# A planned graph and LSTM kernel: weights folded behind the first batches, LSTM states carried through DRAM, buffers freed at a store's landing

## The chip, the cores and the metric

The kernel runs on one core of a Trainium2 chip. The metric is device time in microseconds. The core's engines are TensorE (PE), VectorE (DVE), ScalarE (ACT), GpSimd (POOL), and SyncE (SP), which here only issues DMAs, in order.

## The reference

Inputs are `x` (32 batches of 512 nodes with 128 features, f32), a symmetric 0/1 adjacency `adj` (32 x 512 x 512, ones on the diagonal), and weights. Each of four layers normalises its input over the features (`LN`), takes the relu, and its result is added to its input. Cut to what matters:

```
x1 = x  + softmax over neighbours of relu(q) . relu(k), times relu(v)      # attention
h  = relu(LN(x1));  dyn = conv(h[last 128 nodes]);  lw = LSTM(dyn)          # 128 steps, all batches
x2 = x1 + sigmoid( (D^-1/2 (A + I) D^-1/2 h) @ lw )
n  = relu(LN(x2));  four times: n_i = tanh( A_norm(n W_s..) , n W_n.. , A_norm(n W_d..) ; W_u )
x3 = x2 + n_4
out = x3 + prelu( A_norm (relu(LN(x3)) W^T) + bias )
```

The LSTM runs over 128 steps for all 32 batches at once, each step waiting for the one before. It needs the attention's result for the last 128 nodes of every batch, and the second layer of every batch needs its states `lw`. Since the adjacency is symmetric, the kernel multiplies `W_s`, `W_d`, `W_n` with the blocks of `W_u` beforehand; this product of weights is the *folding*.

## The kernel before

`symmetric` first describes the work as operations and then has a planner order them. There are three stages.

- **First pass** (`pass_1(b)`, ranks 10000 and up): per batch, `LN`, the projections to keys and values, the attention of the last 128 nodes and the convolution. Keys, values and the updated nodes are stored to DRAM (`f_dkq`, `f_dv`, `f_dl`). The convolution's result is written into `f_seq` (128 x 128 x 32).
- **LSTM stage**: `lstm()` has a chain per step: PE products into `f_z` (`L1252`, four quarter matmuls at a time, the "tiled" mode), tanh on ACT (`L1278`, `L1290`), the cell on DVE (`L1284`, `L1285`), tanh of the cell (`L1292`), then the state: `f_h` (`L1296`), transposed in 32 x 32 blocks into `f_seq` (`L1297`). Between the steps `pass_2(b)` does the attention of the other 384 nodes for batches 0 to 27 (`f_pq`, `f_s`, `f_po`). For batches in `EARLY` it loads the whole adjacency, squares it on ACT (`L1389`), forms the second layer's neighbour sums (`f_pg`, in `aggregate`, `L1451`) and stores them (`f_dgT`). Behind batches 4, 7, 10 and 13 of this pass `fold(i)` makes the folded weights of layer `i`.
- **Rest** (`rest(b, turn)`): per batch, the adjacency again, the second layer's gates (`f_pl`), the four message layers (`f_py` `L1548`, `f_pa` `L1451` and `L1559`), the last layer (`f_pg`, `f_p`), the output. The order of turns is `FIRST` (batches 26, 27, begun in the LSTM stage), `NEXT`, then the others by number. The last four batches' `pass_2` lies in this stage.

Before a batch's gates the state is turned: PE transposes `f_seq[:, :, b]` into a PSUM bank `f_plw` (`L1506`), and ACT or DVE copies it to `f_lw` with a factor of 0.5.

The planner (`Plan.run`) gives each operation an engine, a start and an end from costs written into the description, takes at each point the operation that can start first (lowest rank among equals), and emits the instructions in that order; each engine then runs its own in order. Buffers are counted pools (`BUFS`); a new cell has to wait until a slot is free (`free_at`, plus `HOP`). DMAs take their issue time on SP, and `gap` is the extra time until the data can be used. Instruction supply of PE is modelled too: an operation may not start before `FETCH` us after the instruction `AHEAD` places earlier, less `KEEP` places for work that is not an LSTM step:

```
            n = taken[-1] + o.count + (self.KEEP if o.rank >= self.URGENT and self.left else 0) - self.AHEAD
            ...
            return at_time[k] + self.FETCH - o.engines["PE"][0]
```

DMAs issued in the LSTM stage for ranks of 20000 and up also wait for the LSTM step that the plan put before them (`hold_back`).

Of the kernel before, what the change touches and what calls it, by code (L numbers as in the profile page):

```python
# [8 lines left out]
FP = mybir.dt.float32  # L9
AF = mybir.ActivationFunctionType  # L10
OP = mybir.AluOpType
# [510 lines left out]
class Plan:  # L522
# [14 lines left out]
    SWITCH = (0.28, 0.1)  # L537
    AHEAD, FETCH, KEEP = 264, 5.0, 32

# [30 lines left out]
    def op(self, engines, rank, reads=(), writes=(), after=(), gap=0.0, tiled=False, count=8):  # L570

        o = Op()
        o.engines, o.rank, o.no, o.gap = engines, rank, len(self.ops), gap
        o.tiled = tiled
        o.patience = 0.15
        o.count = count
        deps = set(after)
        cells = []
        for acc, is_write in [(a, False) for a in reads] + [(a, True) for a in writes]:
            c, part = acc if isinstance(acc, tuple) else (acc, None)  # L580
            if c not in cells:
                cells.append(c)
            for key, (ws, rs) in c.parts.items():
                if part is None or key is None or key == part:
                    deps.update(ws)
                    if is_write:
                        deps.update(rs)
            mine = c.parts.setdefault(part, ([], []))
            if is_write:
                c.parts[part] = ([o], [])  # L590
            else:
                mine[1].append(o)
        deps.discard(o)
        o.deps = list(deps)
        o.cells = [c for c in cells if c.pool is not None]
        for c in o.cells:
            c.left += 1
        self.ops.append(o)
        return o
# [9 lines left out]
    def run(self, tc, queues):  # L609
# [101 lines left out]
        while done < len(ops):  # L711
# [43 lines left out]
            for c in o.cells:  # L755
                if c not in seen:
                    seen.add(c)
                    slots[c.tag].remove(place(c, s) if c.tag == self.banks else min(slots[c.tag]))
                    if c.tag in self.fifo:
                        turn[c.tag] += 1  # L760
                c.left -= 1
                c.free_at = max(c.free_at, o.end)
                if c.left == 0:
                    slots[c.tag].append(c.free_at)
                    if c.tag == self.banks:
                        unused.append((c.free_at, c.place))
# [22 lines left out]
def symmetric(ctx, tc, x, adj, weights, cols, rows, lstm_b, prelu_a, out, fail):  # L789
# [20 lines left out]
    FIRST = [B - LATE - 2 + k for k in range(2)]  # L810
    NEXT = [22, 23]
    EARLY = range(22)
    FOLDS = (4, 7, 10, 13)
    MOVED = range(2, B - 2)
# [3 lines left out]
    LANDED = 3.8  # L818
    STORED = 5.0
    PATIENCE = 1.3  # L820
    plan_rest = 30_000
    assert D == P and N == 512

    BUFS = {"a": 2, "ar": 6, "x": 7, "xn": 5, "y": 5, "gs": 5, "inv": 4, "n0": 4, "n1": 4, "n2": 4, "n3": 4, "low": 3, "hp": 2, "dt": 2, "mm": 8, "st": 4, "mv": 4, "rs": 4, "sh": 4, "dg": 8, "dv": 4,
            "ri": 3, "th": 3, "c": 3, "cu": 2, "cv": 2, "tcn": 2, "h": 2}
    const = ctx.enter_context(tc.tile_pool(name="f_const", bufs=1))
# [103 lines left out]
    minus_alpha = const.tile([P, 1], FP, name="f_minus_alpha")  # L930
    lb = const.tile([P, 8, TURN], FP, name="f_lb")
    lb_row = const.tile([P, 4, TURN], FP, name="f_lb_row")
# [19 lines left out]
    w_crow = load(HEAD + 12, 64, conv_row, rows[R_CONV].partition_broadcast(P))  # L952
    w_lb = plan.fixed(lb)
    for j in range(P // TURN):
        part = bass.ts(j, TURN)
        DMA(HEAD + 100, 4, lambda part=part: nc.sync.dma_start(
            lb[part], lstm_b.rearrange("s q f -> (s q) f")[:, part].partition_broadcast(TURN)), [], [(w_lb, j)])
    w_lstm = load(HEAD + 100, 512, w[:, W_IH : W_SD[0], :], weights[:, W_IH : W_SD[0], :])
    sd_col = const.tile([P, R_U3 + 1 - R_SD], FP, name="f_sd_col")
    sd_cols = load(HEAD + 100, 5, sd_col, rows[R_SD : R_U3 + 1].rearrange("r p -> p r"))  # L960
    w_last = load(LAST, 64, w_fc, weights[:, W_FC, :])
# [42 lines left out]
    def two_biases():  # L1004
        nc.gpsimd.tensor_add(lb_row, lb[:, :4, :], lb[:, 4:, :])
        for gates in (slice(0, 2), slice(3, 4)):
            nc.gpsimd.tensor_scalar_mul(lb_row[:, gates, :], lb_row[:, gates, :], 0.5)
# [62 lines left out]

    def ln_rstd(rank, mv, a, b, rs):

        def fn():
            nc.gpsimd.tensor_scalar_add(rs[0](), mv.t[:, a:b, 1], EPS_LN)
            nc.gpsimd.tensor_tensor(rs[0](), rs[0](), neg_half[:, 0, a:b], OP.pow)
        POOL(rank, 0.78 + 0.13 * (b - a), fn, [mv], [rs[1]])

# [17 lines left out]

    def ln_full(rank, xc, name, relu=False):
        mv = ln_stats(rank, xc, range(NT), name)
        rs = new("rs", (P, NT), f"f_rs_{name}")
        ln_rstd(rank, mv, 0, NT, (lambda: rs.t[:, :], rs))
        sh = new("sh", (P, NT), f"f_sh_{name}")  # L1100
        ln_shift(rank, lambda: mv.t[:, :, 0], rs, sh, [mv])
        return ln_apply(rank, xc, lambda t: mv.t[:, t, 0:1], lambda t: rs.t[:, t : t + 1], lambda t: sh.t[:, t : t + 1],
                        [mv, rs, sh], name, relu)
# [40 lines left out]
    def pass_1(b):  # L1144
        R = 10_000 + b * 10
        xc = new("x", (P, NT, P), f"f_x_{b}")
        DMA(R, 256, lambda: nc.sync.dma_start(xc.t, x[b].rearrange("(t p) d -> p t d", p=P)), [], [xc],
            gap=2.0 if b == 0 else 4.5 if b < 4 else 3.5)
        al = new("n1", (P, NT, P), f"f_al_{b}")
        DMA(R + 11, 256, lambda: nc.sync.dma_start(al.t, adj[b, :, NR:].rearrange("(t p) i -> p t i", p=P)), [], [al])  # L1150
        xn = ln_full(R, xc, f"a{b}")


# [82 lines left out]


    def lstm():
        last = list(conv_ops)
# [21 lines left out]
        for t in range(T):  # L1261
# [30 lines left out]
            ACT(R, 0.13, lambda tcn=tcn, cn=cn: nc.scalar.activation(tcn.t, cn.t[:, 3, :], AF.Tanh, scale=0.5), [(cn, 2)], [tcn])  # L1292
            h = new("h", (P, TURN), f"f_h_{t}")

            def out_of(th=th, tcn=tcn, h=h, t=t):
                nc.vector.scalar_tensor_tensor(h.t, th.t[:, 4, :], 1.0, tcn.t, OP.add, OP.mult)  # L1296
                return nc.vector.transpose(seq[:, t, :], h.t)  # L1297
            last = [DVE(R, 0.35, out_of, [(th, 1), tcn], [h])]
            steps += last
# [7 lines left out]
    def pass_2(b):  # L1307
# [58 lines left out]
        if early:  # L1366
# [9 lines left out]
            dg = plan.fixed(dram.tile([P, N], FP, tag=f"g{b}", name=f"f_dgT_{b}"))  # L1376
            DMA(R + 5, 256, lambda: nc.sync.dma_start(dg.t, flat(gT.t)), [gT], [dg])
            kept_sums[b] = dg
# [14 lines left out]
    def turned_back(rank, b, a, ar, pieces):  # L1393
# [6 lines left out]
        for k in range(pieces):  # L1400
# [3 lines left out]
            def differ(k=k, at=at):  # L1404
                nc.vector.scalar_tensor_tensor(junk[:, : n * N], flat(a.t[:, n * k : n * (k + 1), :]), 1.0, flat(aT.t[:, n * k : n * (k + 1), :]),  # L1405
                                               OP.mult, OP.not_equal, accum_out=viol[:, at : at + 1])
# [40 lines left out]
    def aggregate(rank, parts, ar, pg):  # L1447
# [15 lines left out]
        return last  # L1463

    def rest(b, turn, lw_after):
        R = 30_000 + turn * 10
# [18 lines left out]
        def norms():  # L1485
# [3 lines left out]
            nc.gpsimd.tensor_tensor(d[:, 0:2, :], d[:, 0:2, :], neg_half, OP.pow)  # L1489
            nc.gpsimd.tensor_scalar_mul(d[:, 2, :], d[:, 0, :], 0.5)  # L1490
            nc.gpsimd.memset(d[:, 3:, :], 0.0)
# [4 lines left out]


        if b in EARLY:
            gT, first = new("gs", (P, N), f"f_gT3_{b}"), None
            gT.ahead = 2  # L1500
            DMA(R, 256, lambda: nc.sync.dma_start(gT.t, kept_sums[b].t), [kept_sums[b]], [gT])
        else:
            gT, first = sums_of_1(R, b, xc, ar, rs)
            diagonal(R, ar, OP.subtract)
        plw = bank(f"f_plw_{b}", (P, P), whole=False)
        PE(R, T_TR, lambda: nc.tensor.transpose(plw.t, seq[:, :, b], ident), [gT], [plw], after=lw_after + ([first] if first else []))  # L1506
        lw = new("low", (P, P), f"f_lw_{b}")
        evict(R, P, lambda: lw.t, lambda: plw.t, [plw], [lw], scale=0.5)
        pl = bank(f"f_pl_{b}", (P, NT, P))
# [11 lines left out]
        moved = turn in MOVED  # L1521
        xn = ln_full(R, xc, f"c2{b}", moved)

# [51 lines left out]
        if turn == B - 1:  # L1575
# [3 lines left out]
            [p4], [xc])  # L1579
        xd = ln_full(R, xc, f"d{b}")  # L1580

# [59 lines left out]
    sum_ops, differ_ops, late, differs = [], [], [], [0]  # L1641
    junk = const.tile([P, 2 * N], BF, name="f_junk")
    for b in range(B):
        pass_1(b)
    end = lstm()
    for b in range(B):
        pass_2(b)
        if b in FOLDS:
            fold(FOLDS.index(b), 20_000 + b * 10)
    for k, b in enumerate(FIRST + NEXT + [b for b in range(B) if b not in FIRST + NEXT]):  # L1650
# [88 lines left out]
```

## Time and profile before

| | us |
|---|---|
| median of 3 runs (1287.78, 1291.28, 1291.68) | 1291.28 |
| profiled execution, its own time | 1290.13 |
| its span, first to last instruction | 1288.3 |
| PE busy | 1259.9 (98%) |
| DVE busy | 985.2 (76%) |
| ACT busy | 834.1 (65%) |
| POOL busy | 386.9 (30%) |
| DMA moved | 232.03 MB, mean 180 GB/s |
| LSTM: first and last transpose into `f_seq` | 181.5 and 497.6 |

The granted TensorE clock was 0.998 in the mean. A busy share is a mean over stages; PE's is besides made from modelled ends of matmuls, which overlap with what follows.

### The profile page before, as it was taken

Reading aid. Unit: us, or ns where it says so; the run is one execution under the profiler, and the core shown is the slowest. Engines: PE = TensorE matmul, PEld = TensorE weight load, DVE = VectorE, ACT = ScalarE, POOL = GpSimd, SP = SyncE. Lnnn points to the kernel's source line nnn. Section 1 sums busy time; section 2 is a strip of 40 time slices with the busy share of each in tenths; the row PEclk is TensorE's granted clock in tenths of the full one; section 3 lists DMA queues with packets and bytes.
Section 4 is the critical chain, followed back from the end, with each engine's and each line's share of the span. In section 5 each row is a group of like instructions: output and inputs, shape, how many; then the busy total and the mean of one; then the engine's idle time right before and its main releaser. Section 6 shows DMA issues by size and latency. Waiting matters only on the chain.

```text
span 1288.3 us, 33017 instructions
## 1 busy us (share of the span) xinstructions
PE 1259.9 (98%) x12085; PEld 971.5 (75%) x12085; DVE 985.2 (76%) x3279; ACT 834.1 (65%) x2092; POOL 386.9 (30%) x733
## 2 busy tenths in 40 slices
PE   8999999999999999999999999999999999999997
PEld 6888876666666667877778787787877877877774
DVE  7889878888878889876677676776776767887654
ACT  5666658777776757764576666666766765676433
POOL 4654523222213216421223232232232322332000
PEclk9999999999999999999999999999999999999999
DMA  8888888868748995877477777776766655673211
GB/s 263 272 273 285 263 263 285 263 208 285 228 138 288 243 272 151 191 165 163 85 164 159 152 164 161 164 150 152 163 162 149 170 116 110 128 173 70 54 25 36
DMA packets 300795, 232.03 MB, mean 180 GB/s; under 512 B 140752, under 2 KB 246224, under 8 KB 300624
## 3 DMA queue, kind: packets, MB, share of 16 engines
q1 hardware_dynamic: 283728, 213.06, 59.9%
q0 software_dynamic: 16896, 16.78, 8.5%
q8 instruction: 97, 1.59, 0.5%
q14 instruction: 74, 0.61, 0.1%
HBM read 136.19 MB, written 62.13 MB: 154 GB/s over the span
## 4 chain that ended last, share of the span: by engine, by line
PE 86%; DVE 7%; ACT 2%; DMA 2%; POOL 1%; issue 1%; DVEq 0%; ACTq 0%; SPq 0%; POOLq 0%
PE f_pa L1451 18%; PE f_py L1548 15%; PE f_pa L1559 15%; PE f_pg L1451 8%; PE f_s L1343 5%; PE f_z L1252 4%; PE f_po L1349 4%; PE f_p L1600 2%; PE f_pk L1159 2%; PE f_pv L1175 2%; PE f_pl L1513 2%; PE f_pol L1202 2%; PE f_sl L1192 2%; PE f_pd L1227 1%; PE f_pq L1334 1%
## 5 line engine op out<-in xcount | busy, mean ns | idle before, releaser
L1451 PE MATMUL f_pa<-f_ar,f_y 128*128 128x512 f32 x1024 | 299.3, 429 | 0.0
L1451 PEld LDWEIGHTS f_pa<-f_ar,f_y 128*128 128x128 f32 x1024 | 189.7, 188 | 73.9 <-issue 40.2
L1548 PE MATMUL f_py<-f_wf,f_n 128*128 128x128 f32 x1280 | 174.0, 275 | 0.0
L1548 PEld LDWEIGHTS f_py<-f_wf,f_n 128*128 128x128 f32 x1280 | 165.3, 191 | 9.4 <-issue 1.9
L1559 PE MATMUL f_pa<-f_n,f_wf 128*128 128x512 f32 x320 | 153.2, 593 | 0.1
L1563 ACT ACTIVATE f_n<-f_pa,f_bcol 128x512 f32<-128x512 f32 x128 | 88.3, 690 | 98.1 <-PE f_pa L1559 98.1
L1434 ACT CAST f_y<-f_py 128x512 fp32r<-128x512 f32 x128 | 74.9, 585 | 95.2 <-PE f_py L1548 90.4
L1389 ACT ACTIVATE f_ar<-f_a 128x512 fp32r<-128x512 f32 x216 | 133.7, 622 | 3.7 <-DMA f_a<-in_adj_dram 2.4
L1396 POOL DMA_DIRECT2D f_das<-f_ar x32 | 26.9, 842 | 350.1 <-ACT f_ar L1389 293.2
L1555 DVE TENSOR_TENSOR f_pa<-f_pa,f_inv 128x512 f32<-128x512 f32 x128 | 86.5, 692 | 28.5 <-PE f_pa L1451 28.3
L1349 PE MATMUL f_po<-f_v,f_e 128*32 128x129 f32 x3072 | 107.4, 273 | 0.4 <-DVE f_e L1347 0.2
L1349 PEld LDWEIGHTS f_po<-f_v,f_e 128*32 128x32 f32 x3072 | 90.2, 110 | 19.8 <-issue 15.3
L1343 PE MATMUL f_s<-f_q,f_k 128*32 128x384 f32 x1024 | 101.7, 486 | 0.0
L1435 DVE TENSOR_TENSOR f_y<-f_py,f_y 128x512 fp32r<-128x512 f32 x128 | 87.5, 685 | 17.4 <-ACT f_y L1434 17.2
L1252 PE MATMUL f_z<-f_w,f_seq 128*32 128x128 f32 x2040 | 83.6, 276 | 12.6 <-issue 5.0
L1559 PEld LDWEIGHTS f_pa<-f_n,f_wf 128*128 128x128 f32 x320 | 57.6, 190 | 45.9 <-issue 37.2
L1252 PEld LDWEIGHTS f_z<-f_w,f_seq 128*32 128x32 f32 x2040 | 53.0, 109 | 48.7 <-issue 16.4
L1405 DVE SCALAR_TENSOR_TENSOR f_junk<-f_a,f_aT 128x1024 bf16<-128x1024 f32 (+1 forms) x68 | 78.5, 1154 | 4.7 <-DMA f_aT<-f_das 3.7
L1114 DVE COPY f_hl_d<-f_n 128x1024 uint16<-128x1024 uint16 x28 | 19.4, 693 | 75.9 <-ACT f_n L1563 75.9
L1451 PE MATMUL f_pg<-f_ar,f_xp_d 128*128 128x512 f32 x256 | 74.1, 413 | 0.3 <-DVE f_xp_d L1443 0.2
L1548 PE MATMUL f_py<-f_wf,f_T_c 128*128 128x128 f32 x448 | 72.9, 275 | 0.0
L1086 ACT ACTIVATE f_xn_c<-f_x,f_sh_c,f_rs_c 128x128 f32<-128x128 f32 x140 | 59.1, 486 | 18.9 <-DVE f_sh_c L1094 18.5
(196 smaller groups left out, 2749.1 us busy)
## 6 DMA issues: line engine op xcount, KB each, us to landing
f_a<-in_adj_dram SPq DMA_DIRECT2D x28, 1024.0 KB
f_a<-in_adj_dram SPq DMA_DIRECT2D x104, 256.0 KB
f_das<-f_ar POOLq DMA_DIRECT2D x32, 512.0 KB, 4.7
f_dkq<-f_kh SPq DMA_DIRECT2D x32, 448.0 KB
f_dv<-f_v SPq DMA_DIRECT2D x32, 258.0 KB
f_v<-f_dv SPq DMA_DIRECT2D x32, 258.0 KB
f_x<-in_x_dram SPq DMA_DIRECT2D x32, 256.0 KB
f_al<-in_adj_dram SPq DMA_DIRECT2D x32, 256.0 KB
```

The costliest lines, as they stand in the source:

```text
L1252: nc.tensor.matmul(z.t[part, k, :, :], h, w[:, m : m + 4, part], start=False, stop=True, skip_group_check=True)
L1343: PE(R, t_mm(NR), lambda s=s, j=j: quarters(lambda p: nc.tensor.matmul(s.t[p], keys.t[:, j * P + p.start : j * P + p.stop], q.t, start=Tru ...
L1349: PE(R, t_mm(P), lambda e=e, t=t, j=j: quarters(lambda p: nc.tensor.matmul(po.t[p, t, :], e.t[:, t * P + p.start : t * P + p.stop], v.t[:, ...
L1389: ACT(rank, 0.62, lambda t=t: nc.scalar.activation(ar.t[:, t, :], a.t[:, t, :], AF.Square, accum_out=deg.t[:, t : t + 1]), [(a, t)], [(ar, ...
L1405: nc.vector.scalar_tensor_tensor(junk[:, : n * N], flat(a.t[:, n * k : n * (k + 1), :]), 1.0, flat(aT.t[:, n * k : n * (k + 1), :]), OP.mu ...
L1434: ACT(rank, t_act(N), lambda: nc.scalar.copy(parts.t[:, :, 0, :], src.t), [src], [(parts, 0)])
L1435: DVE(rank, t_dve(N), lambda: nc.vector.tensor_sub(parts.t[:, :, 1, :], src.t, f32(parts.t[:, :, 0, :])), [src, (parts, 0)], [(parts, 1)])
L1451: nc.tensor.matmul(pg.t, parts.t[:, j, k, :], ar.t[:, j, :], start=(k == 0 and j == 0), stop=(k == 1 and j == NT - 1))
L1548: nc.tensor.matmul(py.t[:, j, :], nodes[n].t[:, bass.ts(j, P)], wf[:, W_F[i] + c, 0, :], start=False, stop=(c == nch - 1), skip_group_chec ...
L1555: before = DVE(R, t_dve(N), lambda pa=pa: nc.vector.tensor_mul(pa.t, pa.t, inv_row.t), [inv_row], [pa])
L1559: nc.tensor.matmul(pa.t, wf[:, W_F[i] + c, 1, :], nodes[n].t, start=False, stop=(c == nch - 1), skip_group_check=True)
L1563: ACT(R, 0.57, lambda pa=pa, n=n, i=i: nc.scalar.activation(n.t, pa.t, AF.Tanh, bias=bcol[:, i : i + 1]), [pa], [n])
```

## The change

- **State.** Four steps' states stay in one tile `f_h` (128 x 4 x 32), which is stored to a DRAM tensor `f_dh` (128 partitions x 128 steps x 32). From turn 8 on, an early batch's state is not turned by PE: a DMA reads it from `f_dh` with the axes exchanged straight into `f_lw`, issued right behind the load of the batch's sums. The factor 0.5 moves into the scale that the gates' tanh already has (0.5 to 0.25).
- **Early batches** are 0 to 23 instead of 0 to 21, and `NEXT` is 24, 25 instead of 22, 23.
- **Folding** is described behind `pass_1` of batches 0 to 3, at their ranks, and its bias columns are loaded at the head.
- **Planner.** A buffer whose last user is a DMA is free only after that DMA's `gap`; the sums' store has `STORED` as its gap, which is 3.5 instead of 5.0; `FETCH` is 4.5 instead of 5.0, `KEEP` 48 instead of 32.
- **Buffers.** `x` has 8 instead of 7, `h` 3 instead of 2; the comparison of the adjacency with its transpose writes over the transpose instead of into a tile of its own (`f_junk`), and the LSTM biases lie in a pool's buffer.
- **Norms.** The addition of the epsilon is done by DVE instead of POOL for batch 0 of the first pass and for both norms of the last turn (`quick`). The first `x` is loaded in two halves.

Cut to its core:

```diff
-    AHEAD, FETCH, KEEP = 264, 5.0, 32
+    AHEAD = 264
+    FETCH = 4.5
+    KEEP = 48
...
-                c.free_at = max(c.free_at, o.end)
+                c.free_at = max(c.free_at, o.end + max(0.0, o.gap))
...
-    NEXT = [22, 23]
-    EARLY = range(22)
-    FOLDS = (4, 7, 10, 13)
+    EARLY = range(24)
+    NEXT = [len(EARLY), len(EARLY) + 1]
+    FOLD_AT = (0, 1, 2, 3)
+    BOUNCED = 8
...
-    STORED = 5.0
+    STORED = 3.5
...
-    w_lb = plan.fixed(lb)
+    w_lb = new("n0", (P, 8, TURN), "f_lb")
...
-    sd_cols = load(HEAD + 100, 5, sd_col, rows[R_SD : R_U3 + 1].rearrange("r p -> p r"))
+    sd_cols = load(HEAD + (0.33 if min(FOLD_AT) < 100 else 100), 5, sd_col, rows[R_SD : R_U3 + 1].rearrange("r p -> p r"))
...
         def fn():
-            nc.gpsimd.tensor_scalar_add(rs[0](), mv.t[:, a:b, 1], EPS_LN)
+            if not quick:
+                nc.gpsimd.tensor_scalar_add(rs[0](), mv.t[:, a:b, 1], EPS_LN)
             nc.gpsimd.tensor_tensor(rs[0](), rs[0](), neg_half[:, 0, a:b], OP.pow)
-        POOL(rank, 0.78 + 0.13 * (b - a), fn, [mv], [rs[1]])
+        if quick:
+            DVE(rank, 0.1, lambda: nc.vector.tensor_scalar_add(rs[0](), mv.t[:, a:b, 1], EPS_LN), [mv], [rs[1]])
+        POOL(rank, 0.78 + 0.13 * (b - a) - (0.25 if quick else 0.0), fn, [mv], [rs[1]])
...
-            h = new("h", (P, TURN), f"f_h_{t}")
+            if k == 0:
+                h = new("h", (P, MANY, TURN), f"f_h_{t}")
...
-            last = [DVE(R, 0.35, out_of, [(th, 1), tcn], [h])]
+            last = [DVE(R, 0.35, out_of, [(th, 1), tcn], [(h, k)])]
+            if k == MANY - 1:
+                DMA(2_000 + t, 64, lambda h=h, t=t: nc.sync.dma_start(dh.t[:, t - k : t + 1, :], h.t), [h], [(dh, t)], gap=STORED)
...
-            DMA(R + 5, 256, lambda: nc.sync.dma_start(dg.t, flat(gT.t)), [gT], [dg])
+            DMA(R + 5, 256, lambda: nc.sync.dma_start(dg.t, flat(gT.t)), [gT], [dg], gap=STORED)
...
+    def state_of(b, lw):
+
+        return nc.sync.dma_start(lw.t.rearrange("t (j f) -> t j f", f=TURN), dh.t.rearrange("(j b) t f -> b t j f", b=B)[b])
...
-            nc.gpsimd.tensor_scalar_mul(d[:, 2, :], d[:, 0, :], 0.5)
+            nc.gpsimd.tensor_scalar_mul(d[:, 2, :], d[:, 0, :], 0.25)
...
-            DMA(R, 256, lambda: nc.sync.dma_start(gT.t, kept_sums[b].t), [kept_sums[b]], [gT])
+            bounced = turn >= BOUNCED
+
+            def sums_and_state():
+                made = nc.sync.dma_start(gT.t, kept_sums[b].t)
+                return state_of(b, lw) if bounced else made
+            DMA(R, 536 if bounced else 256, sums_and_state, [kept_sums[b]] + ([dh] if bounced else []), [gT] + ([lw] if bounced else []))
...
-        plw = bank(f"f_plw_{b}", (P, P), whole=False)
-        PE(R, T_TR, lambda: nc.tensor.transpose(plw.t, seq[:, :, b], ident), [gT], [plw], after=lw_after + ([first] if first else []))
-        lw = new("low", (P, P), f"f_lw_{b}")
-        evict(R, P, lambda: lw.t, lambda: plw.t, [plw], [lw], scale=0.5)
+        if not bounced:
+            plw = bank(f"f_plw_{b}", (P, P), whole=False)
+            PE(R, T_TR, lambda: nc.tensor.transpose(plw.t, seq[:, :, b], ident), [gT], [plw], after=lw_after + ([first] if first else []))
+            evict(R, P, lambda: lw.t, lambda: plw.t, [plw], [lw])
...
     for b in range(B):
         pass_1(b)
+        for i, at in enumerate(FOLD_AT):
+            if at == b:
+                fold(i, 10_000 + b * 10)
```

## The prediction

> **What bounds the kernel now.** I read the stages first, because a mean over the whole span mixes three different limits. Stages cut from the trace: first pass to 179 us, LSTM from 179 to 498 (the 128 transposes into `f_seq` start between 181.5 and 497.6), a transition, the rest stage, the tail. Columns: stretch, its length, then busy us and instruction count of PE, PEld, DVE, ACT, POOL, then clock, DMA share, GB/s.
>
> ```profile
> 0.00:179.00 179.00, 173.86 (x1380) 147.33 (x1384) 150.77 (x672) 113.66 (x226) 94.74 (x245) 1.00 0.87 272
> 179.00:498.00 319.00, 305.57 (x6306) 213.88 (x6300) 266.52 (x1107) 234.01 (x830) 86.56 (x170) 1.00 0.78 241
> 498.00:520.00 22.00, 21.80 (x292) 19.20 (x284) 20.52 (x81) 14.10 (x39) 12.18 (x20) 1.00 0.72 155
> 520.00:1270.00 750.00, 749.91 (x4083) 585.74 (x4082) 539.86 (x1398) 468.00 (x990) 192.13 (x297) 1.00 0.62 136
> 1270.00:1289.00 19.00, 8.75 (x48) 5.31 (x47) 7.53 (x24) 4.35 (x9) 1.27 (x2) 0.87 0.20 60
> ```
>
> PE looks full everywhere. It isn't: the ends of matmuls are modelled and overlap, so I count instructions and multiply by the pace at which equal ones follow each other. The chain of waits, where PE is the chain, gives the paces (start, us, what):
>
> ```profile
> 1242.88 0.93 PE f_pa L1451 x4
> ...
> 1245.65 2.68 PE f_py L1548 x24
> ...
> 1249.23 1.72 PE f_pa L1559 x4
> ...
> 478.62 1.29 PE f_s L1343 x16
> 479.91 0.44 PE f_z L1252 x16
> ```
>
> So an aggregation matmul takes 0.231 us (0.93/4), a 128-column one 0.112, a 512-column f32 one 0.43, a quarter score matmul 0.081, and `f_z` and `f_po` 0.0275. Times the counts of the groups by line in each stage:
> - **Rest**: 1312 aggregation records (303.1) + 448 of `L1559` (192.6) + 2275 of 128 columns (254) + 48 of `f_po` (1.3) = 751 of 750 us. PE has no room; each us of PE work removed here is a us.
> - **LSTM**: `f_po` 76.2 + `f_s` and `f_pq` 98.7 + `f_z` 56.1 + `f_pg` 42.5 + weight folding 9.0 = 282.5 of 319. 36.5 us are lost, in mode switches and stalls.
> - **First pass**: 162.6 us from 7.07 (end of the warm-ups) to 179, which is 172 us; 9.3 lost, 3.8 of them before 32 us (from 7 to 32 us: 10 of `f_pk` and 151 of 128 columns, 21.2 of 25).
>
> The folding's rows and the rest stage's transpose rows (out<-in, count, busy, mean ns, idle before):
>
> ```profile
> L1032 PE MATMUL f_wT<-f_ident,f_w 128*128 128x128 f32 x21 | 3.8, 291 | 0.0
> L1037 PE MATMUL f_pw<-f_w,f_wTs 128*128 128x128 f32 x14 | 3.4, 324 | 0.0
> L1043 PE MATMUL f_pw<-f_w,f_sd_col 128*128 128x128 f32 x16 | 2.4, 275 | 0.0
> L1506 PE MATMUL f_plw<-f_ident,f_seq 128*128 128x128 f32 x32 | 8.8, 276 | 0.0
> ```
>
> What ends last in the LSTM stage: the shortest steps in the timeline take 2.16 us, the mean one 316.1/127 = 2.49. The chain alone would need some 276 us, so neither chain nor PE (282.5) explains 319 alone: PE work stands in the way of steps, and there are stalls. Two kinds show. First, PE stops inside a group of `f_z` that waits for nothing (timeline):
>
> ```profile
> 408.91 0.61 PE L1252 MATMUL f_z<-f_w,f_seq 128*32 128x128 f32 x14
> 411.48 0.27 PE L1252 MATMUL f_z<-f_w,f_seq 128*32 128x128 f32 x1 [1.95 <-issue]
> ```
>
> About 182, 349 and 409 us, 1.4 to 2.0 each. Second, SP's queue stands until a store lands (waited for: us in total, times, longest):
>
> ```profile
> SPq L1329 <- DMA f_dgT<-f_x: 25.9, 10, 4.9
> SPq L1478 <- DMA out_dram<-f_x: 50.6, 22, 4.0
> ```
>
> Once this reaches PE: around 303 us adjacency issues take 4.99 us for six, ACT waits 1.54 for `f_a`, and the next `f_z` starts at 311.10 after 1.52 idle; that step takes 4.12 us.
>
> [...] So an `f_pg` of eight (1.85 us) or a fold standing before `f_z` delays the step; steps with `f_z` 1.0 to 1.3 us late are in the trace. [...]
>
> **The change, part by part.**
>
> *State in place of transposes, rest stage.* Turns 8 to 27 are batches 4 to 23: 20 transposes go, 20 x 0.112 = **-2.2 us** of PE that is full. 20 evictions (0.29, DVE) go too; DVE is at 72% there, worth nothing. Added: 20 loads of 64 KB in 128-byte runs, 512 packets each. The page's q1 averages 0.599 x 16 x 1288 us / 283728 = 0.0435 us a packet; at that, 512 x 0.0435/16 = 1.4 us of all engines per 24 us batch, beside a share of 62%. The trace has no such load; [...] I double it as an upper bound, 2.8 us. Still covered. Their 0.4 us issues stand behind `f_gT`'s on an SP queue that waits for `L1609` 245 us in all. If the state came late, the gates would wait, and PE with them; below nothing there is no gain. I take 0 (0 to +4).
>
> *Stores of states, LSTM stage.* 32 of 64 KB, 512-byte runs: 128 x 0.0435/16 = 0.35 us of DMA and about 0.4 us of SP issue each, 11 and 13 us over 319. DMA (78%) hides them. But each waits on SP for the step's `f_h`, and adjacency loads for ACT's squares queue behind it. I take 0 (0 to +15, priced under the rivals).
>
> *Two more early batches (22, 23).* Two aggregations of eight leave the rest stage: 2 x 8 x 0.231 = **-3.7**. They come into the LSTM stage: +3.7, and 0.5 for two switches of mode. Also there: 2 x 256 KB of adjacency more, two sum stores and last-rows (some 1.2 MB, 4 us at 272 GB/s), eight squares' ACT time and about 4 us of DVE, at 73% and 84%: nothing on the path.
>
> *Folding into the first pass.* PE: 79 matmuls x 0.112 and eight small ones = 9.0 us out of the LSTM stage, with 14 entries into the untiled mode. Around 302 to 304 us a fold's entry and exit leave about 0.25 empty: 3.5. So the LSTM stage gives -9.0 - 3.5 + 4.2 = **-8.3** if PE's work paces it. Range: 0 if it doesn't, -12 if the steps freed run at the chain's pace. In the first pass the 9.0 come back. Weights are 33 blocks of 64 KB, 2.1 MB, 7.7 us at 272 GB/s, queued on SP with the first four `x` loads and ahead of `f_w` for attention. `x` 4 lands by about 11 us now and is needed near 26, so 8 us later is in time; batch 0's key weights come 1.4 us later. Of the 9.0, the holes before 32 us take at most 3.8: +5.2 to +10.5 (the late key weights on top), I take **+7.0**. ACT and DVE work of the folds (7 x 0.9 and 4 x 0.45) moves with them; DVE is at 84% in that stage.
>
> *Head and tail.* The quick norm takes a POOL add of 0.23 to DVE: twice in the tail, **-0.4**. At the head nothing: PE's warm-ups run to 7.07, and the first transposes follow at once.
>
> *Buffers free at landing, fetch 4.5, keep 48, one more `x` and `h`.* They only reorder. One step of 4.12 against 2.2 is a visible loss of 1.9, [...] the plan's new numbers may remove or add such. I take **-1.5** (-6 to +4). `f_junk`'s removal costs no instruction.
>
> Sum: -2.2 - 3.7 - 8.3 + 7.0 - 0.4 - 1.5 = **-9.1**. The profiled execution's own time is 1290.13 (span 1288.3 and 1.8 around it); the median shown is 1291.28, 1.15 above. 1290.13 - 9.1 = 1281.0, and half of that difference gives **1281.5**.
>
> **Rivals.**
> - *The step chain paces the LSTM stage* (chance 0.15). For it: steps of 2.16 show that a step can pass unhindered, and DVE and ACT are in each. Against: 36.5 us lost, much of it just before `f_z`. Then the 8.3 are not given back: 1290.13 - 5.9 + 7.0 - 0.4 = 1291, no change.
> - *SP's queue becomes the wait: slower* (0.20). Each of 32 stores holds SP until its step ends, with adjacency loads behind. Price of one late load: 1.9 us, the step at 307. If eight stores do this, +15, so 1281 + 15 = 1296. It decides from about five, where the gain is used up. For it: SP already stands 25.9 us behind one kind of store. Against: loads in this stage are already tied to LSTM steps, so most waits would have been there.
> - *Holes take the folds and the stalls go* (0.15): first pass +5.2, LSTM -12, reordering -5: 1290.13 - 5.9 + 5.2 - 12 - 0.4 - 5 = 1272.
> - *The bounced state arrives late*, so the change only swaps a wait (within the second rival's chance): 20 x 0.3 us = 6, taking the sum to 1287.
>
> **How the numbers follow.** The likeliest case (0.50) spans 1276 to 1287. About 0.3%, 3.9 us, is what a measurement can tell from no change. Faster by more: 0.15 + 0.50 less its upper edge, 0.65; within: 0.15; slower: 0.20. The range 1270 to 1297 takes in all centres; about 2 in 10 lie outside.
>
> **What would show it.** Right: `f_plw` counts 12; `L1032` to `L1044` stand before 60 us; the rest stage's PE work is 6 us less and still full; the transposes into `f_seq` start 5 to 9 us later and span about 306 us; SP's wait for `f_dgT` at `x`'s load is gone or small. Wrong: the `f_seq` span stays near 316 (chain), or SP waits for `f_h` with ACT's squares waiting for `f_a` (queue), or PE idles before `f_pl` (state late), or the first pass grows by over 9.

## The result, and the profile after

The changed kernel takes 1287.22 us (median of 8, 1283.22 to 1290.37), the kernel before 1291.11 beside it: ratio 0.9967, 95% interval 0.9952 to 0.9981. A second set of runs gave 1284.71 (0.9956, 0.9944 to 0.9968). So it is faster, by 4 to 6 us where 9.1 (ratio 0.993) were forecast. The profiled execution below took 1290.37 (span 1288.6) and is the slowest of its eight; a second profile of the same kernel, called "again", has a span of 1284.3. I use both.

The windows by stage of the kernel after (stretch, length, then busy us and count of PE, PEld, DVE, ACT, POOL, clock, DMA share, GB/s):

```profile
0.00:187.00 187.00, 184.05 (x1447) 157.12 (x1451) 154.03 (x683) 117.37 (x237) 92.06 (x243) 1.00 0.85 269
187.00:504.50 317.50, 305.44 (x6357) 209.94 (x6358) 272.18 (x1139) 237.24 (x834) 101.46 (x186) 1.00 0.83 250
504.50:526.00 21.50, 21.50 (x227) 18.87 (x228) 18.91 (x73) 13.02 (x37) 7.46 (x11) 0.90 0.76 160
526.00:1270.00 744.00, 742.50 (x3995) 578.91 (x3994) 525.03 (x1351) 467.64 (x985) 195.10 (x294) 1.00 0.63 138
1270.00:1289.00 19.00, 9.05 (x47) 5.54 (x45) 8.03 (x26) 4.65 (x9) 1.44 (x1) 0.86 0.20 60
```

The first pass is some 8 us longer, the LSTM stage about as long as before, the rest 6 shorter; and the transition has a clock of 0.90 where it had 1.00. The groups that the change touches (count | busy us, mean ns | idle before):

```profile
L1035 PE MATMUL f_wT<-f_ident,f_w 128*128 128x128 f32 x21 | 3.1, 274 | 0.0
L1040 PE MATMUL f_pw<-f_w,f_wTs 128*128 128x128 f32 x14 | 2.9, 290 | 0.1
L1046 PE MATMUL f_pw<-f_w,f_sd_col 128*128 128x128 f32 x16 | 2.4, 275 | 0.0
L1531 PE MATMUL f_plw<-f_ident,f_seq 128*128 128x128 f32 x12 | 3.1, 285 | 0.0
```

`f_plw` counts 12 instead of 32. The view of one line gives min/median/max ns, then the first and last start: one product of the folds runs at 9.5 to 35.5 us, and the LSTM's transposes span 314.0 us from 190.1.

```profile
L1040 PE MATMUL f_pw<-f_w,f_wTs x14: 275/275/378, 9.5 to 35.5; 128*128 128x128 f32 x14
L1308 DVE STREAM_TRANSPOSE f_seq<-f_h x128: 210/211/214, 190.1 to 504.1; 128x32 f32<-128x32 f32 x128
```

A store's *landing* is the moment when its data has arrived. Of SP's waits, the one for the landing of `f_dgT` fell from 25.9 us to 1.0 (0.5 in "again"); that for the output's stores stayed:

```profile
SPq L1495 <- DMA out_dram<-f_x: 51.0, 22, 3.1
```

**The ledger.** I cut each profile at the first and the last transpose into `f_seq`, count PE's matmuls by line in each piece and take them at the prediction's paces. A piece's length less this work is PE's idle time (warm-ups count as idle, a halved clock too). The pieces add up to 1.0 to 1.1 us more than the span, in every run alike, so the idle time of the rest stands that much too high everywhere and differences are not touched. Work + idle, us:

| | first pass | LSTM | rest | work in all | idle in all |
|---|---|---|---|---|---|
| before | 165.3 + 16.2 | 279.2 + 37.0 | 776.2 + 15.5 | 1220.7 | 68.7 |
| after | 174.4 + 15.7 | 278.4 + 35.6 | 765.7 + 19.8 | 1218.5 | 71.1 |
| again | 174.4 + 14.8 | 278.8 + 35.0 | 765.3 + 17.1 | 1218.5 | 66.9 |

PE's work fell by 2.2, the twenty transposes, as forecast. The folds' 9 us left the LSTM stage, but the stage's work fell by 0.4 to 0.8 only: aggregations (+4.6 and +5.1, of which 3.7 are the two new early batches) and `f_po` (+2.9) moved in from behind the LSTM's end. The rest gave up 10.5 to 10.9 in place of 5.9. That is a shift; only work in all and idle make time. Forecast was 6.9 less idle; it is +2.4 and -1.8.

**Where new idle came from.** DVE, timeline of after (idle before, and what ended it): the comparison of batch 26's adjacency waits for its turning transfer, and a batch norm for an `x` that was stored just before; each has an LSTM cell behind it.

```profile
462.48 0.69 DVE L1418 SCALAR_TENSOR_TENSOR f_aT<-f_a,f_aT 128x512 bf16<-128x512 f32 x1 [2.52 <-DMA f_aT<-f_das]
...
501.88 0.86 DVE L1089 TENSOR_SCALAR f_xn_c<-f_x,f_ln,f_rs_c 128x128 f32<-128x128 f32 x3 [3.06 <-DMA f_x<-f_dx]
```

These LSTM steps take 5.65 and 5.47 us (6.76 and 4.62 in "again"). The chain of waits shows the transfers (start, us): the plan reckons with 7 us for the first, which took 10.27 in "again".

```profile
453.47 8.92 DMA f_aT<-f_das
495.73 6.12 DMA f_x<-f_dx
```

PE's timeline shows the second stop, and the windows around it what it did to the clock:

```profile
502.86 1.51 PE L1356 MATMUL f_s<-f_q,f_k 128*32 128x384 f32 x8 [2.82 <-ACT f_e L1359]
```
```profile
499.00:502.00 3.00, 1.03 (x19) 0.34 (x16) 0.12 (x1) 0.07 (x1) 0.88 (x1) 1.00 0.85 289
502.00:508.50 6.50, 5.64 (x18) 3.45 (x19) 5.24 (x17) 4.32 (x12) 0.00 (x0) 0.51 0.29 89
508.50:512.00 3.50, 3.50 (x20) 3.02 (x19) 2.48 (x7) 1.51 (x5) 0.88 (x1) 0.94 0.36 128
```

After a stop of 2.82 PE ran for 5.6 us at half clock, 2.8 us lost. In "again" the same stop is 1.97 and no clock falls; its rest stage has 2.7 less idle. So the same stop, 0.85 us longer in one execution of the same kernel, went with 2.7 of the 4.3 us between the two spans.

### The profile page after: what moved, and what is told of

It reads as the page before. It is cut to its first block, busy times and chain, and to the rows that moved or that the text cites. A ratio compares the mean times of both kernels' runs of the same rounds, so it can differ in the third digit from the quotient of the medians.

```text
span 1288.6 us, 33047 instructions
## 1 busy us (share of the span) xinstructions
PE 1262.5 (98%) x12065; PEld 970.4 (75%) x12065; DVE 978.2 (76%) x3268; ACT 839.9 (65%) x2100; POOL 397.5 (31%) x734
## 4 chain that ended last, share of the span: by engine, by line
PE 88%; DVE 5%; ACT 2%; POOL 2%; DMA 1%; issue 1%; ACTq 0%; SPq 0%; DVEq 0%; POOLq 0%
PE f_pa L1464 18%; PE f_py L1572 15%; PE f_pa L1583 15%; PE f_pg L1464 8%; PE f_po L1362 4%; PE f_s L1356 4%; PE f_z L1262 4%; PE f_sl L1200 2%; PE f_pol L1210 2%; PE f_pl L1537 2%; PE f_pk L1167 2%; PE f_pv L1183 2%; PE f_p L1624 2%; PE f_pd L1235 2%; PE f_pq L1347 1%
## 5 line engine op out<-in xcount | busy, mean ns | idle before, releaser
L1402 ACT ACTIVATE f_ar<-f_a 128x512 fp32r<-128x512 f32 x224 | 138.5, 620 | 5.3 <-DMA f_a<-in_adj_dram 2.9
L1447 ACT CAST f_y<-f_py 128x512 fp32r<-128x512 f32 x128 | 75.1, 588 | 72.1 <-PE f_py L1572 66.8
L1448 DVE TENSOR_TENSOR f_y<-f_py,f_y 128x512 fp32r<-128x512 f32 x128 | 87.9, 687 | 38.3 <-ACT f_y L1447 36.5
L1362 PE MATMUL f_po<-f_v,f_e 128*32 128x129 f32 x3072 | 112.8, 274 | 2.5 <-issue 2.5
L1418 DVE SCALAR_TENSOR_TENSOR f_aT<-f_a,f_aT 128x1024 bf16<-128x1024 f32 (+1 forms) x68 | 76.4, 1154 | 2.6 <-DMA f_aT<-f_das 2.5
L1464 PE MATMUL f_pg<-f_ar,f_xp_c 128*128 128x512 f32 x256 | 70.8, 417 | 0.3 <-issue 0.3
```

The lines of the kernel that those rows point to most:

```text
L1362: PE(R, t_mm(P), lambda e=e, t=t, j=j: quarters(lambda p: nc.tensor.matmul(po.t[p, t, :], e.t[:, t * P + p.start : t * P + p.stop], v.t[:, ...
L1402: ACT(rank, 0.62, lambda t=t: nc.scalar.activation(ar.t[:, t, :], a.t[:, t, :], AF.Square, accum_out=deg.t[:, t : t + 1]), [(a, t)], [(ar, ...
L1418: nc.vector.scalar_tensor_tensor(flat(aT.t[:, n * k : n * (k + 1), :]), flat(a.t[:, n * k : n * (k + 1), :]), 1.0, flat(aT.t[:, n * k : n ...
L1447: ACT(rank, t_act(N), lambda: nc.scalar.copy(parts.t[:, :, 0, :], src.t), [src], [(parts, 0)])
L1448: DVE(rank, t_dve(N), lambda: nc.vector.tensor_sub(parts.t[:, :, 1, :], src.t, f32(parts.t[:, :, 0, :])), [src, (parts, 0)], [(parts, 1)])
L1464: nc.tensor.matmul(pg.t, parts.t[:, j, k, :], ar.t[:, j, :], start=(k == 0 and j == 0), stop=(k == 1 and j == NT - 1))
```

## The experiments

Times are medians, with the ratio to the kernel before on the same chip and its interval. Idle is from the ledger (before 68.7, again 66.9).

### How much is the order's chance?

Again, the changed kernel unedited: 1284.71, told above.

> The changed kernel once more, for a second profile. If the two long steps of its first profile (5.65 and 5.47 us, where DVE and ACT stand for a DMA) belong to the order, both come again within a few tenths and the LSTM's span from first to last state is 312 to 315 us. If they were an accident of that execution, at least one is below 3 us and the span is 309 to 311. Time 1284 to 1290 either way.

Both long steps came again, so they belong to this order, but not within a few tenths: 6.76 and 4.62 us.

The planner's `HOP`, the time that it assumes for a buffer's return, is moved by 0.01, in the changed kernel (n1) and in the one before (n2). No part of the change is touched, but the order is planned anew.

```diff
-    HOP, URGENT = 0.25, 1000
+    HOP, URGENT = 0.26, 1000
```

> The changed kernel with a planner's number that means nothing on the chip moved a little (0.26 in place of 0.25 us assumed for a buffer's return). Same instructions, another order. If an order's luck decides between these kernels, the time moves by 3 us or more from 1284.7, up or down, and PE's idle time with it. If orders made by the same rules are alike, it stays within 2.

> The kernel before with the same number moved, 0.26 for 0.25. If an order's luck decides: 3 us or more from 1290.7; together with the changed kernel's it says how much of the measured difference may be luck. Otherwise within 2.

n1: 1282.72 (0.9928, 0.9904 to 0.9951), idle 63.5. n2: 1292.95 (1.0006, 0.9994 to 1.0019), idle 70.5. By these ratios an order's chance is about 1 us in the kernel before and 4 to 5 in the changed one; the two kernels stay apart in both orders. No difference of 5 us or less between two orders is read as a cause here by itself.

n1's ratio is the forecast's 0.993. Its LSTM stage has 32.3 us of idle time, 4.7 less than before (35.6 and 35.0 in the changed kernel as built). DVE's waits for transfers in this stage tell the two orders apart (us, times, longest), "again" first, then n1:

```profile
DVE f_aT L1418 <- DMA f_aT<-f_das: 3.6, 1, 3.6
DVE f_xn_c L1089 <- DMA f_x<-f_dx: 2.2, 1, 2.2
```
```profile
DVE f_x L1089 <- DMA f_dx<-f_x: 0.8, 1, 0.8
DVE f_xn_c L1089 <- DMA f_x<-f_dx: 0.3, 1, 0.3
```

n1 has no wait for a turning transfer here, and its longest step is 4.06 us.

### Does the chain of steps pace the LSTM stage?

a7 makes 12 batches early, a6 22 (as before), in the changed kernel:

```diff
-    EARLY = range(24)
-    NEXT = [len(EARLY), len(EARLY) + 1]
+    EARLY = range(12)          # a6: range(22), NEXT as it follows
+    NEXT = [24, 25]
```

> The changed kernel with only 12 early batches: 12 aggregations, 22 us of PE work and some 3 us of mode switches, leave the LSTM stage for the rest stage. If PE's work paces the LSTM stage, as the prediction took it, its span falls by 20 to 25 us, to about 290, and the time is that of the changed kernel within 3. If step chain and in-order queues pace it: the span falls by less than 10, PE stands idle more there, and the time rises by 12 or more.

> The changed kernel with 22 early batches, 22 and 23 next. Two aggregations (3.7 us of PE) go from the LSTM stage to the rest stage. If the LSTM's span is not set by the PE work in it: span within 2 us of 313.8, rest stage +3.7, time +3 to +4. If it is set by PE: span -4, time within 1.

a7: 1290.28 (0.9998, 0.9988 to 1.0009). Its LSTM stage has 18.1 us less PE work and is 14.8 us shorter (299.0 against 313.8), idle 38.3; the rest has 19.5 more work. Neither forecast was met: the span fell by less than 20 and by more than 10, and the time is 5.6 above the changed kernel's 1284.7, between 3 and 12. a6: 1285.68 (0.9962, 0.9951 to 0.9974), LSTM 306.8 for 6.8 us less work. So the stage gives back most of the work that leaves it (14.8 of 18.1, and 7.0 for 6.8), where the chain rival had it give back nothing: that rival falls. Its idle time is 32 to 40 us in all 18 profiles but b1 (51.1) and c1 (45.2), told below. And two more early batches are worth nothing that these runs can tell, as forecast (-3.7 + 4.2).

### The states through DRAM

a4: no state stored, all turned by PE.

```diff
-    BOUNCED = 8
+    BOUNCED = 99
...
-            if k == MANY - 1:
+            if k == MANY - 1 and BOUNCED < B:
```

> The changed kernel with the states neither stored nor loaded: all 32 states turned by PE again. By PE's ledger of the rest stage: 20 transposes of 0.112 come back there, +2.2 us, time about 1287 against 1284.7. If the 32 stores held up SP and the loads behind it in the LSTM stage, the LSTM's span falls by 3 or more below 313.8 and the time stays or falls.

1294.09 (1.003, 1.0016 to 1.0043). PE's work is 1220.7, 2.2 more than in the changed kernel, exactly the 20 transposes; idle is 71.2. The other 4.3 lies in the rest, with a stop of 2.2 us at 569 us. It isn't a price of turning: ahead of the gates' matmuls `f_pl`, PE's starts lag its pace by 0.3 us in all 32 batches together, as against 0.2 in "again". The LSTM's span did fall, by 11.8 us, but 12.0 of work left the stage and its idle time is the same (35.2 against 35.0). So stores and loads cost nothing that shows, and SP's stores as a wait, the slower rival, fall: without them nothing is faster.

### The folding and the plan's numbers

Three kernels from the one before: b1 only moves the folding, b2 only takes the planner's numbers, b3 both. a1 puts the folding back in the changed kernel.

```diff
 b1, b3
+        if b < 4:
+            fold(b, 10_000 + b * 10)
...
-        if b in FOLDS:
-            fold(FOLDS.index(b), 20_000 + b * 10)
 b2, b3
-    AHEAD, FETCH, KEEP = 264, 5.0, 32
+    AHEAD, FETCH, KEEP = 264, 4.5, 48
-                c.free_at = max(c.free_at, o.end)
+                c.free_at = max(c.free_at, o.end + max(0.0, o.gap))
-    STORED = 5.0
+    STORED = 3.5
 a1
-    FOLD_AT = (0, 1, 2, 3)
+    FOLD_AT = (104, 107, 110, 113)
```

> The kernel before, with the folds alone moved behind the first four batches of the first pass (and their bias columns loaded at the head). PE's work is the same, so only idle time can change. If the move is a gain by itself (14 mode switches less in the LSTM stage, holes filled at the head): the first pass +7 to +8, LSTM span and rest together -11 to -13, time 1285 to 1287. If the move only shifts work: first pass +8, the other two -8, time 1289 to 1292. If its price in the first pass is not given back: 1294 or more.

> The kernel before with the planner's new numbers alone (fetch 4.5, keep 48, stored 3.5, a buffer free at the landing). Taking them out of the changed kernel cost 15 us, of which 5.0 was one PE stop at 604 us behind a turning transfer. If foreseen landings are worth that by themselves: 1290.7 - 8 or more, under 1283, and SP's wait for the sums' store goes from 25.9 to under 10. If those 15 us were that one order's bad luck: 1288 to 1295, with SP's wait gone all the same.

> The kernel before, with the folding moved into the first pass (as in b1_fold_front) and with the planner's new numbers (buffers free at landing, STORED 3.5, FETCH 4.5, KEEP 48, as in b2_plan_new). Nothing else of the change. Theory A (the folding moved forward fills the first pass, so that stores land later than the plan holds; it pays only with a plan that reckons with landings): SP's wait for the landing of f_dgT, 28.6 us in b1_fold_front, falls under 10 us, no LSTM step is over 5 us, and the time is 1284 to 1290. Rival B (what pays is room elsewhere: the eighth x buffer, two more early batches, the states out of PE's rest stage): 1295 or more. Sum of the two single runs' differences from before: +17.2 and +2.4, so 1311 if they simply add.

> The changed kernel with the folds behind batches 4, 7, 10, 13 of the second pass, as before. If folding in the first pass costs its full PE price there and the LSTM stage gives little back: the LSTM begins 8 to 9 us earlier, its span grows by 0 to 4 and the time falls by 4 to 8 us, to about 1281. If the stage is paced by PE's work as the prediction took it: it begins 8 to 9 us earlier, the span grows by 10 to 13, and the time rises by 2 to 4, to about 1290.

b1: 1309.11 (1.0149, 1.0097 to 1.0202), idle 85.8, of it 51.1 in the LSTM stage. b2: 1293.89 (1.0019, 1.0006 to 1.0032), idle 70.1. b3: 1289.2 (0.9998, 0.9988 to 1.0008), idle 66.8. a1: 1294.65 (1.0027, 1.0013 to 1.0041), idle 73.3. Alone the two parts cost 17 and 2; together they cost nothing, with 1.9 us less idle and no gain in time. So the move of the folds needs the plan's new numbers. In b2 SP's wait for `f_dgT` is gone, and nothing is gained. a1 met neither forecast: its LSTM stage is 5.6 us shorter than in "again" though the folds are back in it, because the planner left other work for the rest (268.8 us of work against 278.8); its longest step, 5.90 us, comes with a stop and a halved clock shown at the end. What went wrong in b1 stands in SP's waits (us, times, longest), the chain of waits, DVE's timeline and PE's:

```profile
SPq L1329 <- DMA f_dgT<-f_x: 28.6, 13, 4.9
```
```profile
460.22 8.59 DMA f_aT<-f_das
```
```profile
468.84 0.69 DVE L1405 SCALAR_TENSOR_TENSOR f_junk<-f_a,f_aT 128x512 bf16<-128x512 f32 x1 [5.24 <-DMA f_aT<-f_das]
```
```profile
471.01 1.08 PE L1252 MATMUL f_z<-f_w,f_seq 128*32 128x128 f32 x16 [4.61 <-DVE f_seq L1297]
```

DVE waits for a transfer that took longer than planned (8.59 us, 7 reckoned), the cell is queued behind, and PE stops: this step takes 7.27 us. b1's next longest, 5.11 us, has DVE waiting for a store of `f_dx` that took 7.08 us to land. SP's stands for `f_dgT` are not in these two chains; what they add in b1 is not shown. In b3 SP has no wait for `f_dgT`, and no step is over 3.62 us.

### Which of the plan's numbers?

a5 takes all of them out of the changed kernel, c1 only the landing (with `STORED`), c2 only the instruction supply:

```diff
 a5, c1
-                c.free_at = max(c.free_at, o.end + max(0.0, o.gap))
+                c.free_at = max(c.free_at, o.end)
-    STORED = 3.5
+    STORED = 5.0
-            DMA(R + 5, 256, lambda: nc.sync.dma_start(dg.t, flat(gT.t)), [gT], [dg], gap=STORED)
+            DMA(R + 5, 256, lambda: nc.sync.dma_start(dg.t, flat(gT.t)), [gT], [dg])
 a5, c2
-    FETCH = 4.5
-    KEEP = 48
+    FETCH = 5.0
+    KEEP = 32
```

> The changed kernel with the planner's old numbers: fetch 5.0, keep 32, stored 5.0, a buffer free at the end of its store's issue. If the new numbers are worth something by the waits that they foresee: SP's wait for the landing of the sums' store (25.9 us in the kernel before, gone in the changed one) is back with 15 us or more, and the time rises by 2 to 6. If SP's waits lie off the path: the waits come back, the time stays within 1.5.

> The changed kernel with only the landing taken out of the plan: a buffer whose last user is a DMA is free at the issue's end, and the sums' store has no gap (STORED 5.0 for the rest). FETCH 4.5 and KEEP 48 stay. a5_plan_old, with all three old, took 1299.9, 12.6 over the changed kernel. If it is the landing: SP waits 15 us or more for f_dgT's landing and the time is 1295 to 1302. If it is the instruction supply's numbers: 1284 to 1290. If single parts merely reshuffle the order, anything between, without SP's wait as the cause of a long stop of PE.

> The changed kernel with only FETCH 5.0 and KEEP 32 as before; the landing stays in the plan. If the landing is what the changed kernel hangs on: 1284 to 1290, PE's idle time in the rest stage near the changed kernel's 17 to 20 us. If it is these two numbers: 1295 to 1302, with stops of PE inside groups of matmuls that wait for nothing, as before (1.4 to 2.0 us each), or longer.

a5: 1299.87 (1.0076, 1.0049 to 1.0104), idle 82.2, and SP's wait for `f_dgT` ahead of `x`'s load is back with 17.4. c1: 1298.01 (1.0061, 1.0038 to 1.0084), idle 79.7. c2: 1288.47 (0.9991, 0.9974 to 1.0008), idle 66.3. It is the landing. The two fetch numbers make no difference to PE's idle in the profile, an execution of 1285.65; c2's median is 1.3 to 3.8 above the changed kernel's, which is within an order's chance. Of c1's 12.8 us more idle than "again", 10.2 lie in the LSTM stage, and one chain makes most of them. SP's waits, SP's timeline, then DVE's, then PE's:

```profile
SPq L1342 <- DMA f_dgT<-f_x: 10.4, 4, 5.5
```
```profile
421.38 0.42 SPq L1390 DMA_DIRECT2D f_dgT<-f_x  x1
427.43 0.38 SPq L1342 DMA_DIRECT2D f_x<-in_x_dram  x1
427.90 0.44 SPq L1390 DMA_DIRECT2D f_dgT<-f_x  x1
428.44 1.38 SPq L1339 DMA_DIRECT2D f_a<-in_adj_dram  x3
```
```profile
434.92 0.56 DVE L1360 TENSOR_TENSOR f_e<-f_e,f_a 128x384 f32<-128x384 f32 x1 [6.11 <-DMA f_a<-in_adj_dram]
435.40 0.22 DVE L1294 SCALAR_TENSOR_TENSOR f_cu<-f_th 128x64 f32<-128x64 f32 x1
```
```profile
436.85 1.08 PE L1262 MATMUL f_z<-f_w,f_seq 128*32 128x128 f32 x16 [5.77 <-DVE f_seq L1308]
```

The load of `x` takes a buffer from which sums were just stored. The plan calls it free at the end of the issue; it is free when the store has landed, and SP stands until then, from 421.8 to 427.4. The adjacency loads behind it are issued at 428.44, the mask multiply gets its data at 434.92, the cell follows, and this step takes 7.97 us. The windows show the clock's part: PE is at half speed until 439.9.

```profile
430.00:433.00 3.00, 0.85 (x8) 0.16 (x8) 0.00 (x0) 0.17 (x1) 0.89 (x1) 1.00 0.83 217
433.00:440.00 7.00, 3.15 (x48) 2.13 (x52) 4.48 (x14) 1.96 (x7) 0.00 (x0) 0.51 0.78 255
440.00:443.00 3.00, 3.00 (x67) 2.49 (x56) 2.08 (x10) 1.26 (x5) 0.00 (x0) 1.00 0.67 213
```

In a5 the long stop lies elsewhere, in the rest stage: PE waits 4.84 us at 609 us behind ACT, which waits for a turning transfer of the message layer.

```profile
607.18 1.34 ACT L1119 COPY f_T_c<-f_hT_c 128x1024 uint16<-128x1024 uint16 x1 [7.58 <-DMA f_hT_c<-f_hl_c]
```

### The new waits of the changed kernel

a2 makes 24 and 25 early in place of 22 and 23, so the next turns' `x` is long stored; a3 reckons the turning of 26 and 27 at 8 us.

```diff
 a2
-    EARLY = range(24)
-    NEXT = [len(EARLY), len(EARLY) + 1]
+    EARLY = [*range(22), 24, 25]
+    NEXT = [22, 23]
 a3
-... gap=8.0 if b in NEXT else 4.0)
+... gap=8.0 if b in NEXT + FIRST else 4.0)
```

> The changed kernel with batches 22 and 23 next in turn again and 24 and 25 early in their place, so 24 early batches as before. If the last LSTM step is long because the nodes of batch 24 are loaded back right after they were stored: the last step is 2.2 to 2.6 us in place of 5.47, and the time falls by 2 to 4 us. If it is the mass of work at the stage's end: the last steps stay long, time within 1 us.

> The changed kernel with 8.0 in place of 4.0 us planned for the adjacency's turning transfer of batches 26 and 27 too. If DVE standing for that transfer makes a step of 5.65 us: no step near 459 us over 3.5 us, and the time falls by 1.5 to 3. If planned times don't reach the chip: the step stays or moves elsewhere, time within 1 us.

a2: 1287.11 (0.9975, 0.9964 to 0.9987), idle 66.5; no step of the last ten is over 3.4 us, so the late `x` is gone, but not the time. a3: 1282.40 (0.9934, 0.9914 to 0.9954), idle 64.3, of it 32.3 in the LSTM stage. DVE's wait for the turning transfer there (3.6 in "again") is gone, but the step that it aimed at still takes 5.09 (6.76 in "again"). What holds it now is a stop of PE of 1.77 us inside an `f_po` group that waits for nothing the profile shows, with the state queued on DVE behind it; "again" had this stop too (2.11), under the longer wait. So a3 took 1.7 us out of this step; that its 2.3 us of median come from there is likely and not shown. a3 and n1 have the lowest medians of all, 2 us below "again", which is within an order's chance.

### The head

d1 is a3 with the folding one batch later, so that no fold's weights stand ahead of the attention's:

```diff
-    FOLD_AT = (0, 1, 2, 3)
+    FOLD_AT = (1, 2, 3, 4)
```

> The changed kernel with the turning transfers of batches 26 and 27 reckoned at 8 us until they are in (as in a3_turn_gap, 1282.4) and the folding behind batches 1 to 4 of the first pass instead of 0 to 3. Theory (the head pays for fold 0's weights standing ahead of the attention's): the first f_xt_a starts within 0.3 us of the kernel before's 6.90 instead of 8.0 to 8.8, and the time is 1280 to 1282. Rival (the later head is hidden by what follows): 1282 to 1284, the start of the first transpose into f_seq unmoved at 188 to 190.

1287.94 (0.9988, 0.9979 to 0.9997), idle 67.3: slower than a3 by 5.5 us in median, with 3.0 more idle in the profile, all of it in the rest; why is not shown. The first `f_xt_a` starts at 7.93, not 6.9, so most of my theory of the head falls. What it had right is 0.33 us: in "after" and "again" three matmuls of the fold stand between the warm-ups and `f_xt_a`, in d1 none. The chain of waits says where the rest is: twenty equal warm-ups, which stand ahead of it on PE, end late. Before, then after (start, us):

```profile
1.19 5.88 PE f_warm L969 x20
```
```profile
1.19 7.43 PE f_warm L972 x20
```

The first and last of them start 5.5 to 7.05 us apart over all 18 profiles, whatever the kernel; the profile of before has the shortest, after the longest. The traces' clock records move with it: they begin, at full clock, at 4.04 us in before and at 7.18 in after, the other profiles lie between, in the same order in both numbers. In both, a warm-up starts every 0.43 us until then and every 0.22 after it.

## Why the prediction was right and wrong

- **Bound, direction.** Right. PE work that leaves the LSTM stage shortens it: by 14.8 us for 18.1 (a7), by 11.8 for 12.0 (a4). The forecast's range held the time. (The 276 us taken as the chain's own need are the pace of the fastest tenth of the steps; the shortest step of before is 2.02 us and not 2.16. Nothing hangs on it.)
- **-2.2 for the transposes, 0 for states.** Right. Nothing waits for a bounced state; the rival of a late state falls.
- **First pass +7.0.** Right in kind: it came out 7.7 to 8.6 longer, with +9.1 of work. Behind the warm-ups idle fell from 9.3 (16.2 - 6.9) to 7.1 ("again": 14.8 - 8.0, and 0.3 of the fold's work ahead of `f_xt_a`), 2.2 where 2.0 were taken. But the start of `f_xt_a` was 1.1 to 1.9 later, 0.8 to 1.6 of it by the warm-ups. "At the head nothing" holds of the change but for the 0.3 (DVE had the norm 0.5 us earlier and PE didn't use it); the profile that I counted from had a lucky head.
- **LSTM -8.3, with the reordering's -1.5: the step that failed.** The -9.0 + 3.7 is work and came, mostly in the rest. The -3.5 for mode switches (with +0.5 for two early groups) and the -1.5 for reordering should have shown as 4.5 less idle in this stage. It was 1.4 and 2.0. What the traces show in the place of the missing 2.5 to 3.1 us are waits that the new order made and that the forecast had no term for: DVE stood 2.5 and 3.1 us (3.6 and 2.2 in "again") for a turning transfer and for an `x` just stored, each with the LSTM's cell behind it, in steps of 5.65 and 5.47. n1, the same change in another order, has none for the turning and 0.3 for the `x`, and there the stage's idle fell by 4.7; in a3, without the first wait, by 4.7; in a2, without the second, by 3.5. So the price of a fold's exit is not refuted; what had the wrong size is the new order. It is not proven either: b3 has none of these waits and only 2.2 less idle. Time beyond the fastest tenth of before's steps, summed over 127 steps, gives the same picture: ahead of DVE's cell and state some 15 us before, 23 in "again", 16 in n1, 14 in b3; ahead of and in PE's `f_z` some 40, 30, 33 and 26.
- **Rest: idle put at nothing but the tail's -0.4.** It rose by 4.3 and 1.6 us. Of the 2.7 between the two, up to 2.4 is the half clock after the stop of 2.82, most of which falls behind the last transpose; for the other 1.6 no single cause is found.
- **Reordering -1.5 (-6 to +4).** The term's sign was a guess, and its range too narrow for its parts: landing alone is worth 10.8 to 13.3 us in the changed kernel (c1), and in the one before (b2) there is no gain. It isn't a gain to add, but what lets the folding move at all. The stops in which PE waits for nothing the profile shows did not go with the plan's fetch numbers: they sum to 5.0 us before, 3.6 after, 5.3 in "again", 1.0 in c2 with the old numbers and 0.6 in b3 with the new. What makes them is not shown by any run.
- **Tail -0.4.** From the last `f_p` matmul ahead of the final eight to the end: 15.25 in n2, 14.94 in "again", which have nearly the same order there. Consistent, and within the spread of 13.9 to 16.4.
- **Rivals.** The chain (a7), the stores on SP (a4) and the late state fall; the holes took the folds as said, but the stalls went only in part.

Left open: what makes the 32 us of LSTM idle that remain even in n1, how much of n1's 4.7 is the folds' exits, and how much of the 4 to 6 us beyond the 2.2 of work is order's chance. b3 and the changed kernel differ by 2.0 to 4.5 us in median, of which the transposes give 2.2. The eighth buffer for `x` and the third for `h` have no run of their own.

## What to carry to other kernels

Add up an engine's work over the whole program and its idle time separately; work that leaves a stage where a planner can refill it is no gain there. Price a stall that goes as zero to its length, since another wait may stand in its place. A new order brings waits of its own: go through the transfers that it puts shortly before their use and compare the time reckoned with the time measured (7 us against 8.92 and 10.27 here). In c1 a buffer that a store read was free at the landing, 6.0 us after the issue: a plan that leaves this out puts the wait on the queue ahead of the loads behind it, as there from 421.8 to 427.4 us.

## What the hardware showed

- **Seven stops of PE cost twice.** Between head and tail, the 18 profiles have stops of PE up to 2.31 us (among them 1.97, 2.11 and 2.20) with no fall of the clock, and seven of 2.47 to 5.77 with half clock for 3.41 us (three) or 6.83 (four). With the stop of 2.82 in "after" it lasted from 502.11 to 508.94 us. The shortest stop of the seven, 2.47 in a1, went with 3.41 us at half clock:

```profile
467.00:470.80 3.80, 1.49 (x39) 0.89 (x30) 0.50 (x2) 0.34 (x2) 0.24 (x1) 1.00 1.15 309
470.80:474.20 3.40, 3.01 (x29) 1.48 (x33) 3.21 (x13) 1.06 (x4) 0.00 (x0) 0.52 0.61 188
```

- **Warm-ups differ by run.** The same twenty matmuls took 5.5 us in before and 7.05 in after from the first start to the last: a difference of 1.55 us, a quarter to two fifths of the change's gain.
- **Landings.** In c1 a store of sums issued at 421.38 landed 6.0 us later; a turning transfer took 8.92 in "after" and 10.27 in "again".
